# Layer 2 of a two-layer kernel: a new order table that puts three silu activations into one batch, moves the output projection behind it and gives the decays a seventh buffer

## The chip, the cores and the metric

The kernel runs on one core of one Trainium2 chip. The metric is device time in microseconds (us). Before the change the median of 3 runs is 10747.57 us (10746.86 to 10749.43).

## The reference

Two residual layers work on x of 4 x 192 x 128 x 128 in float32. Layer 1 is a convolution block with fractional Fourier transforms; the change does not touch it. Layer 2 normalises x by groups and sends it through a selective state space model along the L = 16384 pixels of each image:

```python
xz = jnp.einsum('blc,ec->ble', seq, in_proj_w)      # seq: LayerNorm of the pixels
xs, z = jnp.split(xz, 2, axis=-1)                   # 384 channels each
u = silu(causal 4-tap convolution of xs + conv_b)
x_dbl = jnp.einsum('bld,kd->blk', u, x_proj_w)      # -> dt (rank 12), B (16), C (16)
dt = jax.nn.softplus(dt @ dt_proj_w + dt_proj_b)
def step(hcar, inp):                                # for each pixel; 384 channels x 16 states
    dA = jnp.exp(dt_t[..., None] * A)
    hnew = hcar * dA + (dt_t * u_t)[..., None] * B_t[:, None, :]
    y_t = jnp.sum(hnew * C_t[:, None, :], axis=-1)
y = (ys + u * Dp) * jax.nn.silu(z)
out = jnp.einsum('bld,cd->blc', y, out_proj_w)
```

## The kernel before, in words

Layer 2 (`layer1` in the code) cuts the 4 images into 128 **chunks** of 512 pixels. The 384 channels are 3 channel tiles j of 128; the 16 states are 8 pairs `sg`. A chunk so has 24 **positions** k = 8j + sg, each with two scans (q = 0, 1) of 128 x 512. The main loop walks positions in order, chunk after chunk. Below, "k22 q1" is the second scan of position 22.

All engines run the order written out by hand (`tc.manual_schedule`), each in order. At a position the loop issues: phase S of the plan, a transposition back for the next position, `sums` of the position three back, phase A, POOL's `inputs` for two positions on, the two scans with phase M inside the first, then phase L. What the plan holds are all steps of the chunk that are not the scans:

```python
for pos, (n, k) in enumerate(order):
    act(pos, "S")
    turned_back(G * (pos + 1))
    sums(*order[pos - LAG])                  # PE, a little later where sg == LAG
    act(pos, "A")
    inputs(*order[pos + 2])                  # POOL, kind O only
    scans(pos, n, k, lambda: act(pos, "M"))  # DVE, ACT, POOL
    act(pos, "L")
```

An entry `(at, phase, step, args)` of `PLAN` says at which position of its own chunk a step is issued. Negative positions lie in the chunk before: `-16` is position 8 of the chunk before, `-46` position 2 of two chunks before. Positions of 24 and more lie in the next chunk (26 is its position 2). I write positions modulo 24 with their phase: 9M is phase M of position 9.

Each scan needs a **decay** exp(dt A) (ACT, line 922) and an input dt u B. `KINDS` says where the latter comes from:
- V: VectorE multiplies it into PSUM (`product`, L943). P: ScalarE scales a transposed copy (`scale`, four activations, L971) and TensorE transposes it back into PSUM (`turned_back`, L986). For both the decay lies in SBUF (`da`, a ring of `BUFS[0]` = 6 buffers): after scan i is issued, the decay six scans on is, into the buffer that scan i just left (`early`).
- O (k2, k8, k14, k17, k22): POOL multiplies the input (`inputs`, L954), and the decay (`op`) goes into one of three PSUM buffers, issued only three scans ahead (`decay_there`).

After the two scans (L1000, DVE) POOL multiplies by C (`hc`, L1013), and TensorE adds up over the states three positions later (`sums`, L1026; `add_skip`, L1041). `evacuate` (L1035, ACT), `turn` (L1051, PE) and `gate` (L1058, DVE) finish a channel tile; `project_out` (L1066, L1069, PE) and `add_x` (L1073, ACT) finish the chunk. Ahead of the scans of a chunk come `to_tokens` (L732, PE), `moments`, `rstd`, `normed` (L746 to L762, ACT), `to_channels` (L771, PE), `channels` (L787, ACT), `conv` (L802, PE), `proj_z` (L807, L814, PE), `silu_u` (L822) and `silu_z` (L829) on ACT, `proj_x` (L837, PE), `xd_out` (L842, ACT), `proj_dt` (L856, PE), `softplus` (L861, ACT), `turn_b` (L875, PE), `b_out` (L880, ACT), `dt_u` (L868, POOL), `dtu_copy` (L903, ACT) and `turned` (L963, PE).

These TensorE steps share five PSUM banks: a step takes the bank that came free first, and its first matmul waits until that bank's last reader is done. SP issues all loads and stores of layer 2 in one queue: the rows of B and C for each pair (`load_b`, `load_c`, 512 KB each), x, the output, and the last column of each scan (`carry`, L1011).

ScalarE has one function table at a time. Silu, softplus and the exp/ln pair are in three tables; `log_exp()` (L711) puts the third back before the next decay. Steps of one table with no decay between them so share a pair of loads.

Of the kernel before, what the change touches and what calls it, by code (L numbers as in the profile page):

```python
# [18 lines left out]
S = 128  # L19
# [4 lines left out]
L = S // 2 + 1  # L24
# [97 lines left out]
def layer0(tc, x, xmid, st2, w):  # L122
# [434 lines left out]

BUFS = 6, 4, 4, 4  # L560

KINDS = ("VPOPVVVP", "OVVPVVOP", "VOVPVPOP")

PLAN = (
    (-44, "M", "load_x"), (-33, "S", "to_tokens", 0), (-33, "A", "to_tokens", 1),
    (-31, "A", "moments", 0), (-31, "A", "moments", 1), (-31, "L", "rstd"),
    (-31, "L", "normed", 0), (-31, "L", "normed", 1), (-30, "L", "to_channels", 0),
    (-29, "L", "channels", 0), (-28, "S", "to_channels", 1), (-27, "A", "conv", 0, 0),
    (-27, "M", "channels", 1), (-26, "S", "conv", 0, 1), (-25, "S", "conv", 1, 0),
    (-25, "A", "conv", 1, 1), (-24, "M", "conv", 1, 2), (-22, "A", "silu_u", 1),  # L570
    (-22, "M", "conv", 0, 2), (-22, "M", "silu_u", 0), (-21, "A", "proj_z", 0),
    (-21, "A", "silu_z", 0), (-20, "L", "conv", 2, 0), (-19, "S", "conv", 2, 1),
    (-19, "A", "conv", 2, 2), (-16, "M", "silu_u", 2), (-13, "S", "proj_x"), (-12, "S", "xd_out"),
    (-10, "M", "proj_dt"), (-10, "L", "softplus", 1), (-10, "L", "softplus", 0),
    (-10, "L", "softplus", 2), (-9, "S", "turn_b"), (-9, "A", "b_out"), (-9, "A", "dbc_out"),
    (-7, "L", "load_b", 0), (-6, "A", "load_c", 1), (-6, "M", "load_b", 2),
    (-5, "S", "load_b", 1), (-5, "M", "dt_u", 0), (-4, "S", "load_c", 0), (-4, "M", "load_c", 3),
    (-3, "M", "turned", 0), (-2, "M", "load_c", 2), (-2, "L", "dtu_copy", 0),
    (-1, "A", "scale", 0, 3), (-1, "M", "scale", 0, 2), (0, "S", "scale", 0, 6),
    (0, "A", "load_b", 7), (0, "A", "scale", 0, 15), (0, "A", "load_b", 6), (0, "L", "load_b", 4),  # L580
    (1, "S", "load_b", 3), (1, "A", "scale", 0, 7), (1, "A", "dt_u", 1), (1, "M", "scale", 0, 14),
    (1, "L", "load_b", 5), (3, "L", "load_c", 4), (4, "S", "turned", 1), (4, "S", "load_c", 5),
    (4, "A", "load_c", 6), (4, "M", "scale", 1, 15), (6, "S", "scale", 1, 7),
    (6, "A", "load_c", 7), (6, "A", "dtu_copy", 1), (6, "M", "scale", 1, 14),
    (7, "M", "scale", 1, 6), (7, "M", "dt_u", 2), (9, "M", "proj_z", 2), (11, "S", "evacuate", 0),
    (11, "S", "proj_z", 1), (11, "S", "turn", 0), (11, "S", "silu_z", 1), (11, "M", "silu_z", 2),
    (13, "L", "dtu_copy", 2), (14, "M", "gate", 0), (16, "S", "turned", 2),
    (17, "S", "scale", 2, 7), (17, "A", "scale", 2, 6), (18, "A", "evacuate", 1),
    (18, "M", "scale", 2, 10), (19, "S", "turn", 1), (19, "M", "scale", 2, 11),
    (19, "L", "gate", 1), (21, "S", "scale", 2, 14), (21, "A", "scale", 2, 15),  # L590
    (25, "M", "load_xr"), (26, "A", "evacuate", 2), (28, "M", "turn", 2), (30, "S", "gate", 2),
    (31, "M", "project_out", 1), (33, "M", "project_out", 0), (34, "A", "add_x", 0),
    (34, "L", "add_x", 1),
)


def layer1(tc, xmid, out, st2, w, n_tok=S * S):
# [5 lines left out]
    LAG = 3  # L603
    AHEAD, H, HC, TURN = BUFS
    NBLK = T // 128
# [687 lines left out]
```

## Time and profile before

| what | before |
|---|---|
| median of 3 runs | 10747.57 us |
| the profiled execution: its own time | 10746.81 us |
| the profiled execution: span | 10744.7 us |
| first and last store of an output chunk is issued (128 stores) | 1467.2 and 10740.7 us: 73.02 us a chunk |
| busy from 5000 to 7000 us: DVE, ACT, POOL, PE | 1949.47, 1948.23, 1951.21, 1916.70 us |
| granted TensorE clock there | 0.99 |
| table loads of ScalarE | 511 at L711, 255 at L822, 128 each at L829 and L861; 1283 ns each |
| POOL waiting for rows of C, 3000 to 9000 us | 56.0 us, 58 times |
| C rows, issue to landing (min, median, max) | 3.5, 4.9, 8.5 us |

A timeline line has the start in us, the length of the whole group, the engine, the line of the code, the operation, what it writes and reads, and how many instructions stand together; in brackets the idle time before it and what ended that. A group's instructions overlap at their ends, so a chain's cost is read from start to start. A line of the waits has who waited for whom, the total in us, how many times, and the longest.

### The profile page before, as it was taken

The numbers are of one execution on the slowest core, as the hardware profiler recorded it, in microseconds if no ns is written. First come the engines' busy times: TensorE is split into PE (matmuls) and PEld (weight loads), VectorE is DVE, ScalarE is ACT, GpSimd is POOL, SyncE is SP. The second block draws the span as 40 slices with busy tenths as digits, with TensorE's granted clock in tenths as the row PEclk, the third lists the DMA queues.
The fourth block names the chain that finished last, engine by engine and source line by source line (L and its number), as shares of the span: only waits on it lengthen the run. The fifth ranks groups of instructions, "written<-read, shape, count | busy, mean of one in ns | idle before, by whom it ended". The sixth has DMA issues, their size and how long they took to land.

```text
span 10744.7 us, 171310 instructions
## 1 busy us (share of the span) xinstructions
PE 9930.4 (92%) x55554; PEld 6885.5 (64%) x55554; DVE 9996.6 (93%) x10439; ACT 9485.3 (88%) x20458; POOL 9234.1 (86%) x4214
## 2 busy tenths in 40 slices
PE   5777799999999999999999999999999999999998
PEld 2444366666666666666666666666666666666666
DVE  6566699999999999999999999999999999999999
ACT  2333199999999999999999999999999999999998
POOL 0000199999999999999999999999999999999999
PEclk8888799999999999999999999999999999999999
DMA  8786844344444344444344344444444444444443
GB/s 217 190 230 174 235 119 121 111 129 121 113 128 122 113 127 122 113 128 121 113 127 121 115 126 121 114 126 121 115 126 121 116 125 122 116 123 124 116 122 98
DMA packets 1353733, 1407.40 MB, mean 131 GB/s; under 512 B 919441, under 2 KB 970886, under 8 KB 1352198
## 3 DMA queue, kind: packets, MB, share of 16 engines
q1 hardware_dynamic: 1332358, 1333.53, 44.1%
q0 software_dynamic: 13312, 50.34, 1.5%
q10 hardware_dynamic: 7168, 12.59, 0.4%
q8 instruction: 442, 7.24, 0.3%
q14 instruction: 453, 3.71, 0.1%
HBM read 1220.68 MB, written 155.32 MB: 128 GB/s over the span
## 4 chain that ended last, share of the span: by engine, by line
PE 45%; ACT 32%; DVE 11%; issue 3%; DMA 1%; POOL 0%; SPq 0%; DVEq 0%; POOLq 0%; ACTq 0%
PE ps L802 17%; PE ps L1026 12%; ACT da L922 9%; DVE h L1000 8%; ACT dbT L971 5%; PE op L986 5%; ACT op L922 3%; ACT L711 3%; DVE op L943 2%; PE ps L1041 2%; ACT dt L861 2%; ACT sT L762 2%; ACT sT L746 1%; PE ps L732 1%; ACT L829 1%
## 5 line engine op out<-in xcount | busy, mean ns | idle before, releaser
L1013 POOL TENSOR_TENSOR hc<-h,c 128x1024 f32<-128x1024 f32 x3072 | 7210.5, 2371 | 251.3 <-DVE h L1000 121.8
L1000 DVE TENSOR_TENSOR_SCAN h<-da,carry,op 128x512 f32<-128x512 f32 x4712 | 5796.3, 1263 | 1.3 <-issue 0.8
L922 ACT ACTIVATE da<-dt,c_A_log 128x512 f32<-128x512 f32 x4864 | 3436.2, 754 | 90.6 <-DVE h L1000 76.9
L1026 PE MATMUL ps<-ident,hc 128*128 128x128 f32 x24576 | 3161.1, 275 | 3.9 <-POOL hc L1013 3.9
L1026 PEld LDWEIGHTS ps<-ident,hc 128*128 128x128 f32 x24576 | 2831.5, 142 | 416.8 <-issue 368.3
L971 ACT ACTIVATE dbT<-ps,bT 128x128 f32<-128x128 f32 x8192 | 2333.7, 423 | 89.5 <-PE op L986 79.3
L802 PE MATMUL ps<-s,wc 128*128 128x512 f32 x4608 | 2159.8, 595 | 0.0
L943 DVE TENSOR_TENSOR op<-ps,b 128x512 f32<-128x512 f32 x2816 | 1896.4, 673 | 15.6 <-ACT ps L903 13.7
L1000 DVE TENSOR_TENSOR_SCAN h<-op,carry,db 128x512 f32<-128x512 f32 x1240 | 1571.3, 1267 | 211.6 <-ACT op L922 207.3
L954 POOL TENSOR_TENSOR db<-dtu,b 128x1024 f32<-128x1024 f32 x640 | 1533.8, 2397 | 4.3 <-DMA b<-dbc 4.3
L986 PE MATMUL op<-ident,dbT 128*128 128x128 f32 x8192 | 1289.6, 277 | 151.7 <-DVE h L1000 75.6
L986 PEld LDWEIGHTS op<-ident,dbT 128*128 128x128 f32 x8192 | 968.6, 141 | 512.0 <-ACT dbT L971 221.6
L802 PEld LDWEIGHTS ps<-s,wc 128*128 128x128 f32 x4608 | 795.1, 190 | 626.0 <-issue 621.4
L922 ACT ACTIVATE op<-dt,c_A_log 128x512 f32<-128x512 f32 x1280 | 937.4, 732 | 3.0 <-DVE h L1000 3.0
L1066 PE MATMUL ps<-yg,c_woT 128*96 128x512 f32 x1536 | 701.2, 592 | 0.0
L711 ACT ACT_TABLE_LOAD x511 | 655.6, 1283 | 9.8 <-PEq L1283 0.7
L512 POOL DMA_DIRECT2D xmid<-xt x64 | 41.8, 653 | 561.4 <-DVE xt L508 435.9
L868 POOL TENSOR_TENSOR dtu<-dt,u 128x512 f32<-128x512 f32 x384 | 493.1, 1284 | 9.3 <-ACT dt L861 9.3
L732 PE MATMUL ps<-gd,xm 97*128 97x192 f32 x2048 | 433.2, 360 | 0.0
L1066 PEld LDWEIGHTS ps<-yg,c_woT 128*96 128x96 f32 x1536 | 236.9, 163 | 273.2 <-issue 273.2
L1041 PE MATMUL ps<-ddp,u 128*128 128x128 f32 x3072 | 405.8, 275 | 0.0
L201 DVE BATCH_NORM_STATS2 st<-xt 96x6 f32<-96x512 f32 x512 | 322.0, 677 | 82.4 <-DMA xt<-in_x 81.2
(178 smaller groups left out, 9742.1 us busy)
## 6 DMA issues: line engine op xcount, KB each, us to landing
c<-dbc SPq DMA_DIRECT2D x1024, 512.0 KB, 5.0
b<-dbc SPq DMA_DIRECT2D x768, 512.0 KB, 4.7
xt<-in_x SPq DMA_DIRECT2D x164, 768.0 KB, 7.8
xmid<-xt POOLq DMA_DIRECT2D x64, 768.0 KB, 6.0
xm<-xmid SPq DMA_DIRECT2D x128, 384.0 KB, 7.2
carry<-h SPq DMA_DIRECT2D x3072, 1.0 KB, 1.9
xr<-xmid SPq DMA_DIRECT2D x128, 384.0 KB, 5.1
out<-xr SPq DMA_DIRECT2D x128, 384.0 KB, 3.1
```

The source lines that it names most:

```text
L711: nc.scalar.preload_act_table_set("natural_log_exp_and_others")
L802: nc.tensor.matmul(g["c", j][0], wc[:, j, k, :], rhs, start=k == 0, stop=k == 5)
L922: nc.scalar.activation(da, got[n]["dt", j], AF.Exp, scale=A[:, j, st : st + 1])
L943: nc.vector.tensor_tensor(dbs[s], g["dp", j][0], g["b", k % NG][:, q, :], ALU.mult)
L954: nc.gpsimd.tensor_tensor(db, _bc(g["dtu", j], 1, G), g["b", sg], ALU.mult)
L971: nc.scalar.activation(t[:, blk, :], g["tu", j][0][:, at], AF.Identity, scale=g["bT"][:, blk, st : st + 1],)
L986: nc.tensor.transpose(db[:, blk * 128 : (blk + 1) * 128], t[:, blk, :], ident)
L1000: nc.vector.tensor_tensor_scan(h[:, q, :], das.pop(s), dbs.pop(s) if db is None else db[:, q, :], 0.0 if ch == 0 else g["before"][:, j, st ...
L1013: nc.gpsimd.tensor_tensor(hc, h, g["c", sg], ALU.mult)
L1026: nc.tensor.matmul(py[:, blk, :], hc[:, q, blk * 128 : (blk + 1) * 128], ident, start=first, stop=sg == NG - 1 and q == G - 1 and blk == N ...
L1041: nc.tensor.matmul(got[n]["py", j][0][:, blk * 128 : (blk + 1) * 128], got[n]["u", j][:, blk * 128 : (blk + 1) * 128], ddp[:, j, :], start ...
L1066: nc.tensor.matmul(po, woT[:, j, t * CH : (t + 1) * CH], g["yg", j], start=j == 0, stop=False)
```

## The change

Only the constants of layer 2 change: `BUFS[0]` (the ring of `da`) goes from 6 to 7, and `PLAN` is another table of the same steps. What is computed stays the same. What the text of the prediction speaks of, by position in the loop:

| step | before | after |
|---|---|---|
| silu_u 1, silu_u 0, silu_z 0 | 2A, 2M, 3A | 3A, 3M, 2M |
| silu_u 2 | 8M | 9M |
| silu_z 1, silu_z 2 | 11S, 11M | 9M, 9M |
| proj_z 0, conv (1, 2) | 3A, 0M | 2M, 2L |
| proj_z 2, proj_z 1 | 9M, 11S | 6L, 7A |
| project_out 1, 0 | 7M, 9M | 11M, 10S |
| add_x 0, 1 | 10A, 10L | 11M, 13A |
| evacuate 0, gate 0 | 11S, 14M | 10A, 13M |
| proj_dt, softplus | 14M, 14L | 13M, 13L and 14S |
| moments, rstd, normed | 17A, 17L, 17L | 16L and 17S, 17S, 17S and 18A |
| scale (2, 6), (2, 7) | 17A, 17S | 17M, 16M |
| scale (0, 7), (0, 15) | 1A, 0A | 23M, 23M |
| load_c 2 | 22M | 1M |
| dt_u 1 | 1A | 1L |

The whole difference:

```diff
-BUFS = 6, 4, 4, 4
+BUFS = 7, 4, 4, 4
 
 KINDS = ("VPOPVVVP", "OVVPVVOP", "VOVPVPOP")
 
 PLAN = (
-    (-44, "M", "load_x"), (-33, "S", "to_tokens", 0), (-33, "A", "to_tokens", 1),
-    (-31, "A", "moments", 0), (-31, "A", "moments", 1), (-31, "L", "rstd"),
-    (-31, "L", "normed", 0), (-31, "L", "normed", 1), (-30, "L", "to_channels", 0),
-    (-29, "L", "channels", 0), (-28, "S", "to_channels", 1), (-27, "A", "conv", 0, 0),
-    (-27, "M", "channels", 1), (-26, "S", "conv", 0, 1), (-25, "S", "conv", 1, 0),
-    (-25, "A", "conv", 1, 1), (-24, "M", "conv", 1, 2), (-22, "A", "silu_u", 1),
-    (-22, "M", "conv", 0, 2), (-22, "M", "silu_u", 0), (-21, "A", "proj_z", 0),
-    (-21, "A", "silu_z", 0), (-20, "L", "conv", 2, 0), (-19, "S", "conv", 2, 1),
-    (-19, "A", "conv", 2, 2), (-16, "M", "silu_u", 2), (-13, "S", "proj_x"), (-12, "S", "xd_out"),
-    (-10, "M", "proj_dt"), (-10, "L", "softplus", 1), (-10, "L", "softplus", 0),
-    (-10, "L", "softplus", 2), (-9, "S", "turn_b"), (-9, "A", "b_out"), (-9, "A", "dbc_out"),
-    (-7, "L", "load_b", 0), (-6, "A", "load_c", 1), (-6, "M", "load_b", 2),
-    (-5, "S", "load_b", 1), (-5, "M", "dt_u", 0), (-4, "S", "load_c", 0), (-4, "M", "load_c", 3),
-    (-3, "M", "turned", 0), (-2, "M", "load_c", 2), (-2, "L", "dtu_copy", 0),
-    (-1, "A", "scale", 0, 3), (-1, "M", "scale", 0, 2), (0, "S", "scale", 0, 6),
-    (0, "A", "load_b", 7), (0, "A", "scale", 0, 15), (0, "A", "load_b", 6), (0, "L", "load_b", 4),
-    (1, "S", "load_b", 3), (1, "A", "scale", 0, 7), (1, "A", "dt_u", 1), (1, "M", "scale", 0, 14),
-    (1, "L", "load_b", 5), (3, "L", "load_c", 4), (4, "S", "turned", 1), (4, "S", "load_c", 5),
-    (4, "A", "load_c", 6), (4, "M", "scale", 1, 15), (6, "S", "scale", 1, 7),
-    (6, "A", "load_c", 7), (6, "A", "dtu_copy", 1), (6, "M", "scale", 1, 14),
-    (7, "M", "scale", 1, 6), (7, "M", "dt_u", 2), (9, "M", "proj_z", 2), (11, "S", "evacuate", 0),
-    (11, "S", "proj_z", 1), (11, "S", "turn", 0), (11, "S", "silu_z", 1), (11, "M", "silu_z", 2),
-    (13, "L", "dtu_copy", 2), (14, "M", "gate", 0), (16, "S", "turned", 2),
-    (17, "S", "scale", 2, 7), (17, "A", "scale", 2, 6), (18, "A", "evacuate", 1),
-    (18, "M", "scale", 2, 10), (19, "S", "turn", 1), (19, "M", "scale", 2, 11),
-    (19, "L", "gate", 1), (21, "S", "scale", 2, 14), (21, "A", "scale", 2, 15),
-    (25, "M", "load_xr"), (26, "A", "evacuate", 2), (28, "M", "turn", 2), (30, "S", "gate", 2),
-    (31, "M", "project_out", 1), (33, "M", "project_out", 0), (34, "A", "add_x", 0),
-    (34, "L", "add_x", 1),
+    (-46, "M", "load_x"), (-32, "A", "to_tokens", 1), (-32, "M", "to_tokens", 0),
+    (-32, "L", "moments", 0), (-31, "S", "moments", 1), (-31, "S", "rstd"),
+    (-31, "S", "normed", 0), (-30, "A", "normed", 1), (-30, "M", "to_channels", 0),
+    (-29, "A", "channels", 0), (-28, "M", "conv", 0, 0), (-27, "S", "to_channels", 1),
+    (-27, "A", "conv", 0, 1), (-27, "M", "channels", 1), (-25, "M", "conv", 1, 0),
+    (-25, "M", "conv", 1, 1), (-23, "M", "conv", 0, 2), (-22, "M", "proj_z", 0),
+    (-22, "M", "silu_z", 0), (-22, "L", "conv", 1, 2), (-21, "A", "silu_u", 1),
+    (-21, "M", "silu_u", 0), (-20, "A", "conv", 2, 0), (-20, "A", "conv", 2, 1),
+    (-18, "M", "conv", 2, 2), (-15, "M", "silu_u", 2), (-13, "S", "proj_x"), (-13, "M", "xd_out"),
+    (-11, "M", "proj_dt"), (-11, "L", "softplus", 2), (-10, "S", "softplus", 0),
+    (-10, "S", "softplus", 1), (-10, "A", "dbc_out"), (-10, "A", "turn_b"), (-9, "M", "b_out"),
+    (-8, "A", "load_b", 0), (-8, "L", "load_c", 0), (-7, "M", "dt_u", 0), (-4, "A", "load_c", 1),
+    (-4, "A", "load_b", 2), (-4, "M", "load_b", 1), (-3, "A", "load_c", 3),
+    (-3, "A", "load_b", 4), (-2, "A", "turned", 0), (-1, "A", "dtu_copy", 0),
+    (-1, "A", "load_b", 7), (-1, "A", "scale", 0, 2), (-1, "A", "scale", 0, 3),
+    (-1, "M", "scale", 0, 7), (-1, "M", "scale", 0, 15), (0, "S", "load_b", 5),
+    (0, "A", "load_b", 3), (0, "L", "scale", 0, 6), (1, "M", "load_b", 6), (1, "M", "load_c", 2),
+    (1, "L", "dt_u", 1), (2, "A", "scale", 0, 14), (3, "L", "load_c", 4), (4, "A", "turned", 1),
+    (4, "A", "scale", 1, 7), (4, "A", "load_c", 5), (4, "M", "load_c", 6), (4, "L", "load_c", 7),
+    (5, "A", "dtu_copy", 1), (6, "A", "scale", 1, 6), (6, "A", "scale", 1, 15),
+    (6, "L", "proj_z", 2), (7, "A", "scale", 1, 14), (7, "A", "proj_z", 1), (8, "M", "dt_u", 2),
+    (9, "M", "silu_z", 1), (9, "M", "silu_z", 2), (10, "A", "evacuate", 0), (11, "A", "turn", 0),
+    (13, "M", "dtu_copy", 2), (13, "M", "gate", 0), (16, "M", "turned", 2),
+    (16, "M", "scale", 2, 7), (17, "M", "scale", 2, 6), (18, "A", "scale", 2, 11),
+    (18, "M", "evacuate", 1), (18, "L", "turn", 1), (18, "L", "scale", 2, 10),
+    (20, "M", "scale", 2, 14), (21, "S", "scale", 2, 15), (21, "A", "gate", 1),
+    (26, "S", "load_xr"), (26, "A", "evacuate", 2), (27, "A", "turn", 2), (29, "A", "gate", 2),
+    (34, "S", "project_out", 0), (35, "M", "project_out", 1), (35, "M", "add_x", 0),
+    (37, "A", "add_x", 1),
 )
```

## The prediction

> **What bounds the kernel now.** I read the busy time by stage first, then who waits, then each engine's timeline over one chunk. In the steady part no engine has room:
>
> ```profile
> 5000.00:7000.00 2000.00, 1916.70 (x11148) 1358.37 (x11149) 1949.47 (x1994) 1948.23 (x4284) 1951.21 (x876) 0.99 0.42 121
> ```
>
> The columns after the length are PE, PEld, DVE, ACT and POOL, busy. All but the weight loads are busy for 96 to 98% of the time, so a chunk of 73.02 us can lose at most some 1.8 us before DVE and POOL are full. What DVE waits for is one thing (waits of DVE, then of PE, 3000 to 9000 us, about 82 chunks):
>
> ```profile
> DVE h L1000 <- ACT op L922: 140.6, 164, 2.0
> ```
>
> ```profile
> PE ps L875 <- ACT dt L861: 81.9, 82, 1.0
> PE ps L771 <- ACT sT L762: 70.2, 82, 0.9
> ```
>
> DVE loses 1.71 us a chunk, twice in each chunk, at scans of kind O, whose decay is issued three scans ahead. Its timeline has the two places, k22 q1 and k2 q1:
>
> ```profile
> 5085.62 1.25 DVE L1000 TENSOR_TENSOR_SCAN h<-op,carry,db 128x512 f32<-128x512 f32 x1
> 5088.37 1.28 DVE L1000 TENSOR_TENSOR_SCAN h<-op,carry,db 128x512 f32<-128x512 f32 x1 [1.50 <-ACT op L922]
> ...
> 5099.44 1.28 DVE L1000 TENSOR_TENSOR_SCAN h<-op,carry,db 128x512 f32<-128x512 f32 x1 [0.39 <-ACT op L922]
> ```
>
> ACT's timeline shows why it is late there:
>
> ```profile
> 5052.83 0.72 ACT L922 ACTIVATE da<-dt,c_A_log 128x512 f32<-128x512 f32 x1 [0.45 <-DVE h L1000]
> ...
> 5054.52 1.28 ACT L829 ACT_TABLE_LOAD   x1
> 5055.82 1.08 ACT L829 ACTIVATE zs<-ps 128x512 f32<-128x512 f32 x2
> 5056.92 1.28 ACT L711 ACT_TABLE_LOAD   x1
> ...
> 5085.50 2.25 ACT L971 ACTIVATE dbT<-ps,bT 128x128 f32<-128x128 f32 x8
> 5087.50 0.84 ACT L922 ACTIVATE op<-dt,c_A_log 128x512 f32<-128x512 f32 x1
> ```
>
> At 5052.83 (k10 q1) ACT has caught up: it waits for a scan. From there on it has more to do than DVE, and DVE must wait at k22 and at k2. So the period is a loop: DVE's work from k2 q1 to k10 q1, then ACT's from k10 q1 to k2 q1.
>
> **Durations, from start to start.** DVE: scan 1.18, product or gate 0.59 (5045 to 5050). ACT: decay 0.62, scale 1.01 (8 instructions in 2.01 from 5093.75), table load with the start of the next step 1.29, silu 0.57, softplus 0.60, moments 0.66 each, rstd 0.56, normed 0.62, evacuate and add_x 0.50, dtu_copy 0.54, channels 0.76 and 0.66, b_out 0.23. PE: eight transpositions of `sums` 0.87, a transposition back 0.43, a pair of conv taps 1.72, project_out 3.43, proj_z 1.72. Between ACT and DVE 0.17 us pass one way (5052.66 to 5052.83) and 0.25 the other.
>
> DVE's whole chunk is 48 x 1.18 + 22 x 0.59 + 3 x 0.59 = 71.39. From k10 q1 to the start of k2 q1 it is 44.84. ACT's steps in that stretch come to 46.33 by these durations (46.6 in the trace). The loop: 71.39 - 44.84 + 46.33 + 0.42 = 73.30; the trace has 73.03 and 73.31 from one chunk to the next. The method is good to 0.3 us.
>
> **What the change takes away.** Written out, the old order has four groups a chunk (silu at 2, 8 and 11, softplus at 14), each with one load there and one back: eight loads. In the new order the O position 2 issues no decay, so silu_z 0, silu_u 1 and silu_u 0 are one group; the three of 9M are one; softplus at 13L and 14S is one. Six loads: 2 x 1.29 = 2.57 us of ACT a chunk, 3.5%.
>
> [...]
>
> **Where the saving lies.** Both loads that go stand at positions 8 to 11, around the place where ACT catches up anyway, and what ACT saves ahead of such a place it spends waiting there. So the loop must be summed anew. In the new order ACT catches up at k13 q0: positions 10 to 12 hold 7 decays and three copies, 5.8 us, against 9.4 us on DVE. Softplus now follows at once (13L). ACT's steps from k13 q0 on:
> - to the decay of k22 q1: 17 decays 10.6, dtu_copy 0.54, the softplus group with two loads and b_out 4.6, moments to normed 3.1, six scales 6.1, evacuate and channels 1.26: 26.2, against 25.96 of DVE: short by 0.23 + 0.42.
> - to the decay of k2 q1: 11.25 more (8 decays, five scales, dtu_copy, channels) is 37.44, against 36.58 of DVE (26 scans, 8 products, 2 gates): short by 0.86 + 0.42 = 1.28.
>
> The loop is 71.39 - 36.58 + 37.44 + 0.42 = 72.67. Against 73.30 that is **0.63 us a chunk**, not 2.57.
>
> **The seventh buffer: nothing.** After scan i, seven ahead instead of six, the decay still takes the buffer that scan i left, so ACT's wait and its order are the same. It helps only a scan that waits for `da`, and DVE's waits have none. A loss is excluded for the same reason.
>
> **What TensorE adds.** PE is never idle but for the two waits shown above, so its order counts. From to_channels 0 to the end of proj_dt the old order takes 61.0 us (5077.53 to 5065.24 a chunk on); its rows sum to 59.9, the new order's to 58.2, since one `sums` and two transpositions back now lie behind proj_dt. ACT's part of that loop, softplus to normed, grows from 12.0 to 13.2 by a scale that now lies in it. This loop is 0.5 shorter too, so it doesn't bind above 72.8. Moved waits:
> - silu_u 1 (3A) stands behind conv (1, 2) (2L). Both engines start from evacuate 2: PE has proj_z and conv, 3.44 + 0.4; ACT has a scale, a load and silu_z, 2.84. ACT waits 1.0 us, which no row of before shows. Behind it stand all decays. The next tight decay is k8 q1: ACT 17.89 + 1.0 from k2 q1, DVE 18.88. So it is just covered; every further tenth costs a tenth. Bounds: 0 and, if PE comes 0.5 late, 0.5; I take 0.13.
> - evacuate 0 (10A) waits for `sums` behind project_out 0 (10S), some 1.4 us. Position 10 to 12 has room for it (above): nothing. Were that room gone, 1.4.
> - The transposition back for k19 q0 waits for scale (2, 6), now behind normed: 0 to 0.4 of DVE, but it comes off the wait at k22. Nothing.
>
> **Queues.** load_c 2 moves from 22M to 1M. It goes out behind the carry of position 0 at about 5096.9, lands 4.9 later at 5101.8, and POOL's product for k2 starts at about 5103.3. Covered by 1.5 us; at the longest landing of 8.5 it would cost POOL 2.1 us, and POOL has about 1.5 to spare. load_c 0 (16L) can hold SP for a POOL product; only carries stand behind it. dt_u 1 goes behind one `hc`: same sum. Nothing. The start is later once: the first proj_x now stands behind the last statistics of layer 1, and four scales instead of two precede the first decays: some 5 us in all.
>
> **Sum.** 0.63 - 0.13 = 0.5 us x 127 chunks = 64 us less, 5 more. Against the profiled execution, 10746.81, that is 10688. It lies 0.76 us under the median, so nothing is corrected for that.
>
> **Rivals.**
> - *More than that.* If ACT's small waits for PE, in the sums of before, go with the new order, DVE is nearly full: 1.3 us x 127 = 165 us, 10587 (floor 1.7 x 127 = 216, 10531). For: ACT has 2.57 us fewer. Against: the sums from k13 still come out short.
> - *No change.* PE sets the loop as it does today with the waits (1.1 us) that its rows do not sum to: 58.2 + 1.1 + 13.2 + 0.3 is 72.8, and with the wait for scale (2, 6) 73.0: 10725 to 10768.
> - *Slower.* Mechanism: silu_u 1 behind conv (1, 2) at position 3. If PE comes to proj_z 0 1.2 us late, ACT waits 2.2 there, and k8 q1 costs DVE 1.2: 0.7 a chunk over today, 10840. It decides from 0.7 us late on. For: PE has only some 0.5 us in hand there, after 22 us of work without a wait. Against: conv (0, 2) and proj_z 0 stand early enough by the rows.
> - *The batch does not form.* A decay between 9M's three steps would bring the loads back; position 9 issues its first decay behind phase M, so 0.02, within "no change".
>
> **Chances.** Forecast (10640 to 10725) 0.49, more 0.17, no change 0.13, slower 0.21. The range goes from 10580 to 10800: it leaves out half of "more" and about half of "slower". About 0.2% (21 us) is what a measurement can tell from no change: faster by that 0.66, within 0.13, slower 0.21.
>
> **What would show it.** Right: loads at L711 near 384 and at L822 near none; DVE's wait for `op` near 1.2 us a chunk, still at k2 and k22; ACT waiting for a scan at k13, for PE about 1 us ahead of silu_u at position 3; PE's wait at L875 gone, that at L771 grown. Wrong: DVE waiting at k8 or k11 (PE sets the pace), POOL waiting longer for C, or DVE without waits.

## The result and the profile after

| what | before | after |
|---|---|---|
| median | 10747.22 us (4 runs, 10731.74 to 10749.43) | 10993.39 us (4 runs, 10986.08 to 10999.7) |
| ratio, with its 95% interval | | 1.0233 [1.022, 1.0246] |
| the profiled execution: own time, span | 10746.81, 10744.7 us | 10991.69, 10989.6 us |
| first and last store of an output chunk | 1467.2 and 10740.7 us: 73.02 us a chunk | 1485.3 and 10985.6 us: 74.81 us a chunk |
| a chunk in the steady part (mean by the stores from 3000 to 9000 us) | 73.20 us | 75.09 us |
| granted TensorE clock, 5000 to 7000 us | 0.99 | 0.95 |
| table loads at L711 | 511 | 384 |

The changed kernel is 2.3% **slower**; 0.55% less had been forecast. Between the first and the last store lie 227 us of the difference, 1.79 us a chunk; in the steady part it is 1.89. The other 18 come ahead of the first store. In the runs with the new table that store comes anywhere from 1466.7 to 1494.5 us, so the 5 us that the prediction has for a later start can't be seen. The batch did form. The page's group of the loads behind each batch has three a chunk instead of four:

```profile
L711 ACT ACT_TABLE_LOAD x384 | 492.7, 1283 | 7.5 <-PEq L1283 0.7
```

All the same no engine got fuller; the same stretch as in the prediction (PE, PEld, DVE, ACT, POOL busy, then the clock) shows every engine but the weight loads busy for less of the time:

```profile
5000.00:7000.00 2000.00, 1904.00 (x10868) 1384.37 (x10867) 1919.09 (x1946) 1840.06 (x4104) 1902.29 (x854) 0.95 0.40 117
```

The stretch holds 2.5% fewer chunks. POOL fell by as much, DVE by 1.6%, and ACT by more (1948 to 1840), as a kernel with fewer loads should. PE fell by less, to 1904 where 2.5% less would be 1868: it is busy for longer in each chunk. The clock of 0.95 would explain that. Who waits, 3000 to 9000 us (80 chunks; total, times, longest):

```profile
PE op L986 <- DVE h L1000: 253.2, 76, 3.3
...
DVE h L1000 <- PE op L986: 143.9, 239, 1.0
...
ACT u L822 <- PE ps L802: 67.4, 80, 0.8
...
ACT op L922 <- DVE h L1000: 41.6, 77, 1.0
...
DVE h L1000 <- ACT op L922: 25.9, 105, 0.5
```

DVE's large wait is no longer for ACT's decays, but for PE's transpositions back (L986): 1.8 us a chunk. And PE itself has one wait of 3.3 us a chunk, at the same line. The two waits of before that the prediction shows (turn_b for softplus, to_channels 0 for normed, 1.0 and 0.9) are gone.

They were not the only ones. The waits of before from 3000 to 9000 us have two more lines of PE, at the very line that now waits for 3.3 us:

```profile
PE op L986 <- ACT dbT L971: 44.8, 34, 1.5
```
```profile
PE op L986 <- DVE h L1000: 33.8, 33, 1.5
```
```profile
5001.06 0.90 PE L986 MATMUL op<-ident,dbT 128*128 128x128 f32 x4 [1.33 <-ACT dbT L971]
```

In 56 of the 82 chunks of before, PE waits for 1.3 us at the transposition back for k19 q0. So PE stood still for some 1.0 + 1.3 + 0.8 = 3.1 us in such a chunk, in three parts. The prediction's "never idle but for the two waits" left the third out; its timeline was taken from one of the other 26 chunks. In the changed kernel about the same sum, 3.3 us, is one wait. PE's timeline has it, and what follows:

```profile
5023.69 1.04 PE L1026 MATMUL ps<-ident,hc 128*128 128x128 f32 x8
5028.06 1.25 PE L986 MATMUL op<-ident,dbT 128*128 128x128 f32 x4 [3.33 <-DVE h L1000]
5029.10 1.92 PE L1026 MATMUL ps<-ident,hc 128*128 128x128 f32 x8
...
5035.44 0.60 PE L986 MATMUL op<-ident,dbT 128*128 128x128 f32 x4
```

The same eight transpositions of `sums` are 1.04 us long at 5023.69, and 1.92 at 5029.10. The bracket names a scan, which had freed the PSUM buffer; that was not the last condition. The weight load of the same step names the scaled copy (`dbT`). Scale (2, 6), behind normed 0 (5027.02), is the first four of the eight at 5027.64; its first result is there at 5028.01, and PE starts at 5028.06:

```profile
5028.06 0.96 PEld L986 LDWEIGHTS op<-ident,dbT 128*128 128x128 f32 x4 [3.57 <-ACT dbT L971]
```
```profile
5027.64 2.17 ACT L971 ACTIVATE dbT<-ps,bT 128x128 f32<-128x128 f32 x8
```

Now PE alone in slices of 1 us (length, PE busy with its matmuls, granted clock, DMA share, GB/s), first after, then the same kind of place in before:

```profile
5026.00:5027.00 1.00, 0.00 (x0) 1.00 0.00 0
5027.00:5028.00 1.00, 0.00 (x0) 0.58 0.00 0
5028.00:5029.00 1.00, 0.94 (x4) 0.50 0.64 233
...
5033.00:5034.00 1.00, 1.00 (x6) 0.51 0.00 0
5034.00:5035.00 1.00, 1.00 (x12) 1.00 0.20 17
```

```profile
5067.00:5068.00 1.00, 1.00 (x5) 0.69 0.15 35
5068.00:5069.00 1.00, 1.00 (x4) 0.50 0.00 0
5069.00:5070.00 1.00, 1.00 (x6) 0.50 0.15 1
5070.00:5071.00 1.00, 1.00 (x7) 0.60 0.00 0
```

Within PE's long wait the clock falls to 0.5 and stays there until 5033.98, though PE works without a break from 5028.06. What PE does from there to 5035.44 takes 7.38 us. The same steps take 5.10 at full clock in run 7 below: 2.3 us lost. (By the rows they sum to 4.4, but the first transposition also waits for its copies, one after the other, in both.) In ten chunks from 5000 to 5730 us the changed kernel has such a stretch of 6.83 us in every chunk, 68 us together; before has one of 3.41 us in five of the ten, 17 us. From 3000 to 9000 us it is in 26 of the 82 chunks of before, just those in which PE does not wait at k19 q0. Chunks without a slow stretch take 73.03 us there, chunks with one 73.32 (medians). So little, it seems, because the slow work mostly uses up the 1.3 us in which PE would stand still.

So the period now goes through PE's slow work. The waits give the way round: PE runs from the transposition at 5028.06 to the conv that silu_u 1 waits for (5058.66, 0.84 us), but for one wait of 0.24; ACT from there to the decay that k8 q1 waits for (5072.09, 0.27); DVE on to the scan k12 q1, for which ACT waits (5086.37, 0.53); ACT on through softplus and normed to scale (2, 6), and PE's next transposition at 5103.15. The first part is 30.60 us, the rest 44.49. In run 7, at full clock, they are 28.31 and 44.60: the whole difference lies in PE's part.

### The profile page after: what moved, and what is told of

It reads as the page before. It is cut to its first block, busy times and chain, and to the rows that moved or that the text cites. A ratio compares the mean times of both kernels' runs of the same rounds, so it can differ in the third digit from the quotient of the medians.

```text
span 10989.6 us, 170157 instructions
## 1 busy us (share of the span) xinstructions
PE 10093.3 (92%) x55554; PEld 7153.3 (65%) x55554; DVE 10082.5 (92%) x10439; ACT 9210.5 (84%) x20204; POOL 9236.0 (84%) x4214
## 5 line engine op out<-in xcount | busy, mean ns | idle before, releaser
L1000 DVE TENSOR_TENSOR_SCAN h<-da,carry,op 128x512 f32<-128x512 f32 x4712 | 5862.5, 1266 | 301.8 <-PE op L986 213.8
L922 ACT ACTIVATE da<-dt,c_A_log 128x512 f32<-128x512 f32 x4864 | 3378.6, 752 | 13.3 <-DVE h L1000 8.7
L1026 PE MATMUL ps<-ident,hc 128*128 128x128 f32 x24576 | 3282.5, 281 | 5.8 <-POOL hc L1013 5.8
L1026 PEld LDWEIGHTS ps<-ident,hc 128*128 128x128 f32 x24576 | 2933.4, 146 | 314.8 <-issue 290.1
L971 ACT ACTIVATE dbT<-ps,bT 128x128 f32<-128x128 f32 x8192 | 2287.2, 403 | 154.4 <-PE ps L963 154.4
L802 PE MATMUL ps<-s,wc 128*128 128x512 f32 x4608 | 2131.6, 593 | 0.9 <-ACT s L787 0.9
L986 PE MATMUL op<-ident,dbT 128*128 128x128 f32 x8192 | 1379.2, 295 | 449.3 <-DVE h L1000 428.7
L986 PEld LDWEIGHTS op<-ident,dbT 128*128 128x128 f32 x8192 | 1051.0, 149 | 881.5 <-ACT dbT L971 529.3
L1035 ACT COPY yt<-ps 128x512 f32<-128x512 f32 x384 | 224.9, 586 | 303.4 <-PE ps L1026 303.3
L807 PE MATMUL ps<-s,wz 128*128 128x512 f32 x768 | 419.8, 628 | 30.1 <-ACT yt L1035 30.0
```

Of the source, the lines that this page charges most:

```text
L802: nc.tensor.matmul(g["c", j][0], wc[:, j, k, :], rhs, start=k == 0, stop=k == 5)
L922: nc.scalar.activation(da, got[n]["dt", j], AF.Exp, scale=A[:, j, st : st + 1])
L971: nc.scalar.activation(t[:, blk, :], g["tu", j][0][:, at], AF.Identity, scale=g["bT"][:, blk, st : st + 1],)
L986: nc.tensor.transpose(db[:, blk * 128 : (blk + 1) * 128], t[:, blk, :], ident)
L1000: nc.vector.tensor_tensor_scan(h[:, q, :], das.pop(s), dbs.pop(s) if db is None else db[:, q, :], 0.0 if ch == 0 else g["before"][:, j, st ...
L1026: nc.tensor.matmul(py[:, blk, :], hc[:, q, blk * 128 : (blk + 1) * 128], ident, start=first, stop=sg == NG - 1 and q == G - 1 and blk == N ...
```

## The experiments

Three theories stood at the start. **A**: the long idle stretch drops PE's clock, and the slow work behind it makes PE the bound. **B**: it is the wait for the late scale (2, 6) as such, through the transposition to DVE; the clock is an accompaniment. **C**: the loss comes from the rest of the change, the silu batch and the output projection behind it. Each run was compared with the kernel before on the same chip; ratios are to it. A "slow piece" is a stretch at clock 0.5, counted in ten chunks from 5000 us on where nothing else is said; "of 82" counts the chunks from 3000 to 9000 us. Lines of code in these traces are shifted by 65 to 85, since the table is written one entry a line.

**1. Scale (2, 6) one position earlier** in the changed kernel, ahead of moments:

```diff
-(17, "M", "scale", 2, 6),
+(16, "M", "scale", 2, 6),
```

> The changed kernel with one entry moved: scale (2, 6) at 16M, right behind scale (2, 7), so that the transposition back for k19 q0 finds its input ready. Theory A (TensorE stands idle for 3.3 us ahead of k19 q0, its granted clock then falls to 0.5 for 6.4 us, and TensorE sets the period of 75.1 us): the idle time only moves on to to_channels 0, which waits for normed 1 behind the same ScalarE work, so the clock falls as before: 74.5 to 75.5 us a chunk, 10900 to 11030 us. Rival B (the wait for this one scale is the price by itself, without the clock): 1.6 to 3.3 us a chunk come back, 10570 to 10790 us. Rival C (the output projection at 10S and 11M makes TensorE late): no change, 10970 to 11010 us.

Measured: 10771.79 us, 1.0031 [1.0016, 1.0046]. One entry of the table brings 222 of the 246 us back. PE still waits 2.8 us a chunk, but in three parts: 1.71 for the scan that frees the PSUM buffer, 0.18, and 0.91 at to_channels 0, as in before. The first two stand in one line:

```profile
PE op L1051 <- DVE h L1065: 153.3, 161, 1.8
```

Slow pieces: 3.41 us long, in 6 of 10 chunks. A's detail failed: I had expected the remaining wait to keep the clock down as before. B came out with the right time. That PE's idle time hardly shrank (from 3.3 to 2.8) while the slow time went from 68 to 20 us speaks for the clock. The chunks of this run say more: of 82, the 55 without a slow piece take 72.88 us and the 27 with one 74.52 (medians). The scale comes equally early in both, so the 1.6 us between them are not its.

**2. The normalising stretch as in before**, with the batch, the projection behind it and the seven buffers kept (proj_dt to turn_b, moments to channels 0, the scales and turned of tile 2, evacuate 1, turn 1 and gate 1, with to_tokens and dt_u 0, at their old positions):

```diff
-(-32, "L", "moments", 0), (-31, "S", "moments", 1), (-31, "S", "rstd"), ...
-(-11, "M", "proj_dt"), (-11, "L", "softplus", 2), ...
-(17, "M", "scale", 2, 6), (18, "M", "evacuate", 1), ...
+(-31, "A", "moments", 0), (-31, "A", "moments", 1), (-31, "L", "rstd"), ...
+(-10, "M", "proj_dt"), (-10, "L", "softplus", 1), ...
+(17, "A", "scale", 2, 6), (18, "A", "evacuate", 1), ...
```

> The changed kernel with the old places of the steps from proj_dt to channels (proj_dt 14M, softplus 14L, turn_b 15S, to_tokens 15S and 15A, scale (2, x) 17S to 21A, moments 17A, normed 17L, evacuate 1 18A, dt_u 0 19M); the silu batch, the output projection behind it and seven decays ahead stay. Theory A: TensorE's idle time is back to two waits of 1 us, the clock is low for some 2.8 us a chunk: 72.4 to 73.1 us a chunk, 10670 to 10760 us. Rival B: the same. Rival C (output projection): stays at 10950 to 11030 us.

Measured: 10883.37 us, 1.0129 [1.0112, 1.0146]; nobody had that. The clock is 1.00 (one slow piece in ten chunks), and a chunk still takes 74.2 us. The waits tell why:

```profile
DVE h L1065 <- ACT op L987: 170.7, 164, 2.0
ACT dt L926 <- PE ps L921: 138.6, 81, 2.1
```

Softplus waits 1.7 us a chunk for proj_dt, because project_out 0 and 1 (6.9 us of PE) now stand between, at positions 10 and 11. ACT's run to k22 starts that much later, and DVE waits for the decay at k22 as in before, only longer. So C has a true part: with the batch and the output projection behind it, a chunk costs some 1.1 us more than in before, unless proj_dt and softplus come a position earlier, which the changed kernel does. How much of it is the projection's alone was not measured. PE waits for 0.81, 1.11 and 0.94 us here, 2.9 a chunk, nearly as long as in the changed kernel but in three places, and the clock stays up.

**3. Only the late scale, in the kernel before**:

```diff
-(17, "A", "scale", 2, 6),
+(18, "S", "scale", 2, 6),
```

> The kernel before with one entry moved: scale (2, 6) at 18S, behind normed, so that the transposition back for k19 q0 waits on ScalarE. Theory A: TensorE idles some 2.5 to 3 us in one piece and runs slowly after it for 5 us or more: 74 to 75.5 us a chunk, 10870 to 11060 us. Rival B: 1 to 2 us a chunk, 10870 to 11000 us, at a granted clock of 0.97 as before. Rival C: no change or below 10770 us.

Measured: 11103.36 us, 1.0336 [1.0321, 1.0352]; clock 0.96 from 5000 to 7000 us. One entry makes the loss in the old table too, with slow pieces in every chunk (51 us in ten), and a PE wait at the same line:

```profile
PE op L1051 <- ACT dbT L1036: 313.3, 79, 4.3
```

C can't be the main cause. A and B both expected a loss; it is 43 us above A's range and 103 above B's. The clock is as A has it: 0.948 over the whole execution, against 0.972 in before. How much the 4 us of waiting cost here by themselves is not separated from the clock.

**4. Keep PE at work through the wait**, with the scale as late as in the changed kernel: to_tokens 1 is done twice, and two 128x512 matmuls are written into the tile of k19 q0 before its transposition back overwrites them. That adds about 3 us of PE work to each chunk.

```diff
+(-31, "S", "again"),      # to_tokens 1 once more
...
                 db = dbs[at] = psa.tile([128, T], F32, name="op")
+                if (k, q) == (19, 0):
+                    for _ in range(2):
+                        nc.tensor.matmul(db, wc[:, 0, 0, :], wc[:, 0, 0:4, :]..., start=True, stop=True)
                 for blk in range(NBLK):
                     nc.tensor.transpose(db[:, blk * 128 : ...], t[:, blk, :], ident)
```

> The changed kernel with useless matmuls in TensorE's gap: to_tokens 1 is computed a second time at 17S (the same values, 1.3 us), and two matmuls of 128x512 write the PSUM buffer of the transposition back for k19 q0 ahead of it (1.7 us) and are overwritten by it. The output is the same; TensorE has 3 us a chunk more to do. Theory A: the idle time ahead of k19 q0 falls from 3.3 to about 0.5 us, the granted clock stays at 1.00, and 3 to 5 us of TensorE time come back: DVE and ScalarE set the period, 72.3 to 73 us a chunk, 10650 to 10750 us. Rival B: no change, 10970 to 11010 us, since the wait for the scale stays. Rival C: no change or slower, 10970 to 11400 us.

Measured: 10721.45 us, 0.998 [0.997, 0.9989]. More work on the engine that sets the pace, and 272 us less. No slow piece is left. B and C are out as the main cause: the scale is as late and the rest of the change is there.

**5, 6, 7. The parts of the fill**: only to_tokens 1 twice (5); only the two matmuls (6); in their place 16 transpositions, which are overwritten too (7).

```diff
+                if (k, q) == (19, 0):
+                    for i in range(16):
+                        nc.tensor.transpose(db[:, i % 4 * 128 : (i % 4 + 1) * 128], wc[:, 0, 0, :], ident)
```

> The changed kernel with the second computation of to_tokens 1 at 17S alone: the gap ahead of k19 q0 shrinks from 3.3 to 2.0 us in one piece. Theory A, refined by the runs so far (the low clock comes in pieces of 3.4 us, whenever an idle stretch fills enough of a window that runs free of the program): fewer or shorter low pieces than the 6.8 us in each chunk of the changed kernel: some chunks with one piece, 10730 to 10880 us. If only the length of the idle time itself counts (each idle us costs one): 10900 to 10960 us.

> The changed kernel with the two overwritten matmuls ahead of the transposition back for k19 q0 alone: 1.6 us idle, then 1.7 us of matmuls. Theory A: few low pieces, 10720 to 10850 us. If only the idle time itself counts: 10900 to 10960 us; if matmuls at the end of the gap come too late to hold the clock: 10950 to 11000 us.

> As the run before, with 16 transpositions (1.7 us) in the place of the two matmuls. [...] If TensorE's activity of any kind counts: as the run before, within 40 us.

Measured, in this order: 10818.98 us, 1.0064 [1.0049, 1.0079], slow pieces of 3.41 us in 5 of 10 chunks (48 of 82; chunks with one take 74.27 us, without 72.88); 10720.26 us, 0.9973 [0.9962, 0.9984], none; 10717.88 us, 0.9971 [0.9961, 0.998], none. In 7 PE waits 1.62 us, for the scan, then does the fill, and scale (2, 6) is there:

```profile
5052.55 1.97 PE L1052 MATMUL op<-ident,wc 128*128 128x128 f32 x16 [1.62 <-DVE h L1070]
5054.35 1.03 PE L1056 MATMUL op<-ident,dbT 128*128 128x128 f32 x4
...
5059.45 0.60 PE L1056 MATMUL op<-ident,dbT 128*128 128x128 f32 x4
```
```profile
5000.00:7000.00 2000.00, 1948.26 (x11620) 1398.67 (x11618) 1973.09 (x2004) 1888.73 (x4214) 1957.00 (x881) 1.00 0.43 121
```

This is the decisive pair. In 7 the transposition back comes as late against ACT's work as in the changed kernel, since the fill takes the time in which PE stood still (1.62 + 1.80 against 3.33): 11.29 us after softplus (5043.06 to 5054.35), against 11.21. What differs is the clock, 1.00 against 0.95, and with it 10718 against 10993: **275 us, 2.2 us a chunk (72.91 against 75.09), is the price of the clock alone**. From the transposition at 5054.35 to the one at 5059.45 it is 5.10 us, against 7.38: these 2.3 us are where it is paid. DVE goes from 1919 to 1973 busy of 2000.

**8. Both: the early scale and to_tokens 1 twice.**

```diff
-(17, "M", "scale", 2, 6),
+(16, "M", "scale", 2, 6),
+(-31, "S", "again"),
```

> The changed kernel with scale (2, 6) at 16M and the second computation of to_tokens 1: the idle time of 1.7 us that the first experiment left falls to about 0.5 us. Theory A: no low clock, 72.5 to 73.0 us a chunk, 10680 to 10740 us, a little faster than the kernel before. If the low pieces of the first experiment did not matter: 10760 to 10790 us.

Measured: 10757.61 us, 1.001 [1.0, 1.0019]. Missed by 18 us: the waits are down to 0.41, 0.18 and 0.91, but one slow piece in ten chunks is left, 14 of 82. Chunks with one take 74.55 us, those without 72.91, as in run 7: the slow pieces are the miss, 1.6 us x 14 of 82, some 36 us over 127 chunks.

**9. The batch alone, in the kernel before, at position 11**, with the same two loads a chunk fewer and the output projection where it was:

```diff
-(-16, "M", "silu_u", 2), (-13, "S", "proj_x"), (-12, "S", "xd_out"), (9, "M", "proj_z", 2),
+(-13, "M", "silu_u", 2), (-12, "S", "proj_x"), (-11, "S", "xd_out"), (10, "L", "proj_z", 2),
```

> The kernel before with the silu batch alone, put at position 11: silu_u 2 goes from 8M to 11M behind silu_z 2, so two table loads a chunk go as in the changed kernel; for it proj_x moves to 12S, xd_out to 13S and proj_z 2 to 10L; the output projection and six decays ahead stay. By the loop of the prediction (ScalarE's run from k10 q1 to k2 q1) the loads that go lie ahead of the run and one silu of 0.57 us comes into it: 73.6 us a chunk, 10790 to 10850 us, in spite of 2.57 us less on ScalarE. If fewer table loads are time by themselves: 10400 to 10600 us.

Measured: 10902.92 us, 1.0143 [1.0128, 1.0158]; I had the direction, but 50 us too little. What the two loads give back, ACT spends waiting for scans, 3.6 us a chunk, and DVE waits for decays at k22 and k2 more than in before (2.3 against 1.7 us a chunk):

```profile
ACT da L987 <- DVE h L1065: 290.4, 258, 3.0
DVE h L1065 <- ACT op L987: 189.0, 165, 2.0
```

Two loads fewer bring nothing where they stand; the longer waits at k22 and k2 fit a later start of ACT's run to them. Why it is 50 us more than the sum has was not looked into.

**10. Run 7 with six buffers**, `BUFS = 6, 4, 4, 4`:

> The changed kernel with the 16 filling transpositions and six buffers of da in the place of seven. The seventh buffer changes no order and no wait, so the time is that of the run with seven, 10718 us, within 20 us. If the seventh decay ahead is what keeps VectorE from waiting for da: 10740 us or more, and a wait for da in VectorE's list.

Measured: 10724.12 us, 0.9976 [0.9967, 0.9985], the same as run 7 within 7 us. The seventh buffer does nothing that shows.

**11. PE work into the 1.0 us wait of the kernel before**, to see what its own slow pieces cost: the last matmul of proj_dt four times.

```diff
-                nc.tensor.matmul(g["d", j][0], dtT[rows, :], g["xd"][rows, :], start=True, stop=True)
+                for _ in range(4 if j == 2 else 1):
+                    nc.tensor.matmul(g["d", j][0], dtT[rows, :], g["xd"][rows, :], start=True, stop=True)
```

> The kernel before with three more matmuls a chunk: proj_dt of the third tile is computed four times (the same values, 1.1 us), which fills the 1.0 us that TensorE waits for softplus. The trace of before has a low clock for one piece of 3.4 us in about every second chunk, and chunks of 73.31 and 73.03 us. Theory A: the pieces go, and all chunks take some 73.0: 10715 to 10740 us. If the clock does nothing there: 10740 to 10760 us.

Measured: 10996.39 us, 1.0229 [1.0214, 1.0244]. The fill was too long. The three matmuls of proj_dt overlap in the trace of before (starts 0.007 us apart) and take 1.07 us together, from start to start. The three more took 2.57 us (5017.54 to 5021.18 is 3.64 for all six), where I had counted 1.1. By the code the three read different rows of `xd` and the repeats the same; that this makes the difference is not shown. Softplus waits for them:

```profile
5017.54 3.71 PE L922 MATMUL ps<-xd,c_dtT 12*128 12x512 f32 x12
```
```profile
ACT dt L929 <- PE ps L922: 110.9, 79, 2.2
```

A later start of softplus costs here: chunks without a slow piece take 74.28 us, against 73.03 in before. And slow pieces doubled, 34 us in ten chunks, although PE was busier: see the last section. What the slow pieces cost the kernel before, this run doesn't tell. By the chunks of before it is 0.29 us each (73.32 against 73.03), some 0.1 us a chunk on the mean.

**12. Run 7 with the first batch rearranged** (conv (1, 2) before proj_z 0, silu_u 1 and 0 before silu_z 0, scale (0, 15) moved out of the tight stretch), meant to take the 0.84 us wait for silu_u off:

```diff
-(-22, "M", "proj_z", 0), (-22, "M", "silu_z", 0), (-22, "L", "conv", 1, 2),
-(-21, "A", "silu_u", 1), (-21, "M", "silu_u", 0), (-1, "M", "scale", 0, 15),
+(-22, "M", "conv", 1, 2), (-22, "M", "proj_z", 0), (-22, "M", "silu_u", 1),
+(-22, "M", "silu_u", 0), (-21, "A", "silu_z", 0), (2, "A", "scale", 0, 15),
```

> The changed kernel with the 16 filling transpositions, and with two things moved that the sums of ScalarE's run name: conv (1, 2) ahead of proj_z 0 at 2M with silu_u 1, silu_u 0 at 2M and silu_z 0 at 3A (ends the wait of 0.84 us of silu_u 1), and scale (0, 15) from 23M to 2A (1.0 us less ahead of k2 q1). By the sums VectorE's waits fall from 0.7 to about 0.4 us a chunk: 72.2 to 72.7 us, 10630 to 10700 us. If another wait takes their place: 10700 to 10760 us.

Measured: 10731.64 us, 0.9981 [0.9971, 0.9991]; no gain over run 7. In run 7 DVE waits for decays at k22 q1 (0.3 us) and k8 q1 (0.2); here both waits are 0.3, and evacuate 2 waits 1.0 us for PE. The best version stays run 7, 0.3% under the kernel before, by means of PE work that nobody reads.

## Why the prediction was wrong

**The failed step** is the third of the moved waits: "The transposition back for k19 q0 waits for scale (2, 6), now behind normed: 0 to 0.4 of DVE, but it comes off the wait at k22. Nothing." The wait is 3.33 us of PE, where before had 1.3 in 56 of 82 chunks and the prediction had read none. As a wait it does cost nothing: run 7 is as late there, and is fast. But I took PE's idle time for free time, and the sum has no term for the clock. Put together in one place the idle time took the clock down for 6.83 us, and that cost 2.2 us a chunk.

With it fell the sentence on PE's loop, "0.5 shorter, so it doesn't bind above 72.8". From to_channels 0 to the end of proj_dt it is 60.1 measured, against 58.2 by the rows. Run 7 takes 59.25 for it at full clock: 0.8 of the 1.9 is the clock, and 1.1 is what the rows missed in before too (61.0 against 59.9). The rest of the loss lies ahead of to_channels 0: from softplus to it are 14.81 us, against 13.47 in run 7 (5043.06 to 5056.53). ACT's part, softplus to the end of normed, is 13.6 (5016.85 to 5030.43) against the 13.2 of the prediction; but to_channels 0 comes 1.2 later, at 5031.66, since PE has the slow work to do first.

The trace of before had the warning: clock 0.50 to 0.69 from 5067 to 5071, right behind a wait of 1.0 us, and so in 26 of 82 chunks. I had read the mean, 0.99, and gone on. The pieces are 3.41 us long, or twice that, but no wait has to be as long: 1.01 us stood ahead of the fall at 5067.38 in before, and in the changed kernel the clock fell 2.4 us into the wait (5024.73 to 5027.16).

**The rivals.** None had it. The slower one, 10840, had another mechanism (silu_u 1 behind conv (1, 2)); that wait came out at 0.84 where 1.0 was forecast, at position 3, and did little harm. "No change" had PE as the bound, but at full clock: 72.8 to 73.0 us a chunk and 10725 to 10768 us. With the clock held up (runs 4, 6 and 7) that is close to what was measured, 72.9 us and 10718 to 10721.

**What held:** six loads a chunk (384); ACT catching up at k13, or one scan ahead of it: it waits for the scan k12 q1 (41.6 us, 77 times, for the decay in `op`); evacuate 0 waiting 1.47 for PE (1.4 forecast) at no cost; turn_b's wait gone; the seventh buffer worth nothing (run 10); and that loads saved ahead of a place where ACT waits bring nothing (run 9). ACT's own loop, forecast at 72.67, is near what is left when the clock is held up: 72.87 and 72.91 in runs 4 and 7. Whether it is this loop or PE's that sets them is not shown. They give 22 and 32 us less than before where 59 had been forecast: some 0.2 of the 0.5 us a chunk came true.

**The signs.** To_channels 0 waiting longer did not come: that wait is at the transposition ahead of it. DVE's wait for `op` is 0.3 us a chunk, not 1.2, and 0.5 in run 7. It is at k22 q1 and, in place of k2, at k8 q1, which the prediction had named as a sign of being wrong (0.27 us, behind silu_u 1's wait of 0.84; the sum has 0.13 for it). Of the other signs of being wrong, POOL waits longer for C, 81.6 us against 56.0; but in run 7, with the same loads, it is 23.3, so load_c 2 at 1M is not what makes the kernel slow.

## What to carry to other kernels

Idle time of TensorE was not all alike here: 3.3 us a chunk in one wait went with 68 us at clock 0.5 in ten chunks (the changed kernel), 2.9 in three waits with 3.4 us (run 2). So when an order is changed, ask not only how long PE waits but whether its waits now lie together, and look at the granted clock in slices of a microsecond, not in the mean. Work that nobody reads, put into such a wait, tells in one run whether the wait or the clock is the cost. Where a trace has two kinds of chunks, compare them: here they priced the clock without another run. And time that ACT saved ahead of a place where it waits anyway brought nothing (run 9: two loads a chunk fewer, 1.0143 of the time); sum an engine's load from there to the next place where others wait for it.

## What the runs showed of the hardware

**The slow pieces lie on a fixed grid.** Each is 3.41 us long, or twice that, and within a run every start lies a whole number of 3.413 us after the first, to within 0.01 us (before and after from 3000 to 9000 us; runs 1, 3, 5, 9 and 11 from 5000 to 5730): in before at 5067.38, 5214.16, 5432.61, 5579.38 and 5726.15, that is 43, 107, 150 and 193 steps. The changed kernel's pieces start at 5027.16, 5102.25, 5177.34 and so on, 22 steps apart at 2000 as at 9500 us. Its chunk is 75.09 us, exactly 22 steps: it has locked onto the grid. That it did so because the slow work makes the next wait start at the same place of the grid is argued, not shown.

**Active rows fit better than busy time, but not everywhere.** In run 11 PE was busy for the whole of each window of the grid ahead of its 52 falls to 0.5 (3200 to 9000 us), by the trace, but mostly with proj_dt's matmuls of 12 rows. I weighed each matmul's time with its rows over 128. The windows ahead of a fall then hold about 0.27 to 0.35 in the changed kernel, 0.36 to 0.42 in before, up to 0.43 in run 3 and 0.10 to 0.40 in run 11; those without a fall 0.71, 0.40, 0.40 and 0.42 at least. Before fits too: its 1.0 us wait alone left 70% of the window busy, but proj_dt's 12 rows lay in it as well. In the changed kernel the clock stayed low through windows that were 0.63 to 0.78 busy and came back after full ones. Run 5 falls after windows of 0.40 to 0.53. Runs 1 and 8 don't fit: they fall after windows of 0.59 to 0.67, and run 1 has windows of 0.44 without a fall. What sets these apart stays open, and no run changed the rows alone. That a window is weighed at all was the theory ahead of run 5; what the runs show is the grid and these shares.

**Transpositions held the clock up as matmuls did.** Runs 6 and 7, with 1.8 us of matmuls or of transpositions in the same place, are alike: 10720 and 10718 us, no slow piece in either.
